# One-hot rows by pairs, padded relations, and repeated products in layer 0 of a four-layer graph network

## The chip, the core and the metric

The kernel runs on one core of one Trainium2 chip, in one launch. The metric is the device time of a run in microseconds; the median of three runs before the change is 5142.12 us. In the text PE is the tensor engine (products; PEld its loads of weights), DVE the vector engine, ACT the scalar engine, POOL the GpSimd engine, and SP the engine that issues plain DMAs.

## What is computed (the reference)

A graph of 3125 nodes with 128 features and 100,000 edges, sorted by their destination, goes through four layers. Each has the form x = layernorm(x + layer(x)). Cut to what matters here:

```python
# layer 0: attention over edges with relation types (500 relations, 64 numbers each), 8 heads
pre_edge = (h @ P1)[dst] + (h @ P2)[src] + (z @ P3)[edge_type]
logit_edge = leaky(pre_edge) @ y_w
alpha = softmax of the logits over the edges of a destination and the node itself
t_edge = (h @ Wh)[src] + (z @ Wz)[edge_type]
out = leaky(sum over edges of alpha * t_edge + residual_weight * h)
# layer 1: mean over neighbours, summed at the SOURCE of each edge, then two dense layers
agg = segment_sum(x[dst], src) / max(count of edges by src, 1)
# layers 2 and 3: attention with gathered keys and values
```

Layers 2 and 3 are not touched by the change.

## The kernel before, in words

The nodes are ordered by their number of incoming edges and cut into 25 tiles of 128, one node per partition. CAP gives the number of edge slots of each tile (57 down to 21, in all 821), W = 8 is a chunk of slots.

**Layer 0, the attention** (in tile_gnn, from about line 740). For each tile and each chunk of 8 slots, POOL gathers the rows of the source nodes into hs (one indirect DMA per slot, line 90; 8 buffers). Then one of two ways is taken, chosen by by_matmul. In gathered (line 801) the relation rows zs are gathered as well and added, and PE transposes the sum into pre (L815). In multiplied (line 819) the relation rows are made on PE: DVE compares a row of relation numbers with the partition numbers (oh, L834, bf16, 4 x 512), PE multiplies this one-hot with the table zq (L838) into zps, ACT copies it to zT (L839), PE multiplies zT with the weights into pre (L841) and adds the transposed hs (L843). The table zq holds the relation vectors in three bf16 parts, so that their sum is exact to fp32: parts 0 and 1 are one stationary operand of 128 columns, part 2 one of 64. In both ways logits (line 784) follows for each half chunk: DVE adds h1T (low, L787), ACT takes the relu (L788), PE multiplies by yw8 (lg, L790, four products). PE also makes t_ps (L849), which DVE adds to hs (L850). When all chunks of a tile are there, DVE does the softmax and the weighted sum over slots (L872, L796 to L799, L874), and the end of the tile makes x1 and its layer-1 product u.

**Layer 0, the counts.** Beside the attention runs the preparation of layer 1: counts (line 554) makes for each tile a 128 x 3200 matrix of how often each source node occurs. It is a generator, advanced by a share of its steps after each chunk. Its slots are first permuted: DVE makes one-hots ohb (L596) and oha (L600), ACT scales oha (L604, L605), PE multiplies them (c_perm, L608). Then, seven times per tile, DVE makes two blocks of one-hots, ohs and ohd (L623), by comparing numbers with the row up; PE multiplies them, 128 columns at a time (c_ps, L628), and ACT copies the result to cs (L630). All these one-hots are laid out as [partition, value, slot]: the 128 values of one slot lie 8 or 12 elements apart. The row c_up, made by count_up (line 539), holds the values 0 to 127, each 8 times, and fills one bank of PSUM (2 KB per partition).

The code is written in a framework that has its own scheduler: it decides the order of the instructions on each engine, from the dependencies and from priorities in the order of the program. It also sets all waits. It treats two accesses of different engines to the same PSUM bank as dependent, even where their bytes are apart. Each engine then takes its instructions in the built order.

Of the kernel before, what the change touches and what calls it, by code (L numbers as in the profile page):

```python
# [18 lines left out]
P = 128  # L19
# [15 lines left out]
R = 64  # L35
HC = 2 * D + H
NK = (PADREL + 1) // P
# [38 lines left out]
def tile_gnn(ctx, tc, a, out):  # L76
    nc = tc.nc
    V, A, G, T = nc.vector, nc.scalar, nc.gpsimd, nc.tensor
# [457 lines left out]
    V.tensor_copy(each_j, digits[:, :NT].unsqueeze(2).to_broadcast([P, NT, max(CAP)]))  # L536
    NAX = NT * max(NB)

    def count_up(pool, ps):

        up = ps.tile([P, P, SG], BF16, name="c_up")
        of = up.rearrange("p d s -> p (d s)")
        ri = pool.tile([P, 1], I32, name="c_ri")
        V.tensor_copy(ri, rowid)
        V.tensor_scalar(ri, ri, 3, None, op0=OP.arith_shift_right)
        rf = pool.tile([P, 1], F32, name="c_rf")
        V.tensor_copy(rf, ri)
        for k in range(SG):
            row = pool.tile([P, P], BF16, name="c_row", bufs=2)
            V.tensor_scalar(row, onesb, rf, float(k * P // SG), op0=OP.mult, op1=OP.add)  # L550
            T.transpose(of[:, k * P:(k + 1) * P], row, identb)
        return up

    def counts(t, cp, ps, up):

# [36 lines left out]
        perm = ps.tile([P, 2 * NAX], F32, name="c_perm", tag="c_ps")[:, :2 * NA]  # L592
        for s0 in range(0, n, SG):
            k = min(SG, n - s0)
            ohb = cp.tile([P, P, SG], BF16, name="c_ohb", bufs=2)
            V.tensor_tensor(ohb[:, :, :k], digb[:, 0, s0:s0 + k].unsqueeze(1).to_broadcast([P, P, k]),  # L596
                            up[:, :, :k], op=OP.is_equal)
            oha = cp.tile([P, SG * 2 * NAX], BF16, name="c_oha")[:, :SG * 2 * NA]
            oha = oha.rearrange("p (s e a) -> p s e a", s=SG, e=2)
            V.tensor_tensor(oha[:, :k, 1, :], digb[:, 1, s0:s0 + k].unsqueeze(2).to_broadcast([P, k, NA]),  # L600
                            digits[:, :NA].unsqueeze(1).to_broadcast([P, k, NA]), op=OP.is_equal)
            for s in range(k):
                o = OFF[t] + s0 + s
                A.activation(oha[:, s, 0, :], oha[:, s, 1, :], AF.Copy, scale=srclo[:, o:o + 1])  # L604
            A.activation(oha[:, :k, 1, :], oha[:, :k, 1, :], AF.Copy, scale=rowid)  # L605
            yield
            for s in range(k):
                T.matmul(perm, ohb[:, :, s], oha[:, s].rearrange("p e a -> p (e a)"), start=(s0 + s == 0),  # L608
                         stop=(s0 + s == n - 1))
        ends = cp.tile([P, 2, NAX], BF16, name="c_ends")  # L610
        V.tensor_scalar(ends[:, 0, :NA], perm[:, :NA], -1.0, None, op0=OP.add)
        A.activation(ends[:, 1, :NA], perm[:, NA:], AF.Copy)
        cs = cp.tile([P, NP], BF16, name="c_sb")
        for c in range(NCW):
            w = min(CW, NP - c * CW)
            n2, e0 = nb * w // P, nb * CW // P * c
            yield
            ohs = cp.tile([P, P, SE], BF16, name="c_ohs", bufs=2)
            ohd = cp.tile([P, P, SE], BF16, name="c_ohd", bufs=2)
            for b0 in range(0, n2, SG):  # L620
                b1 = min(n2, b0 + SG)
                for to, end in ((ohs, 0), (ohd, 1)):
                    V.tensor_tensor(to[:, :, b0:b1], ends[:, end, e0 + b0:e0 + b1].unsqueeze(1)  # L623
                                    .to_broadcast([P, P, b1 - b0]), up[:, :, :b1 - b0], op=OP.is_equal)
            cps = ps.tile([P, CW], F32, name="c_ps")
            for j in range(w // P):
                for i in range(nb):
                    T.matmul(cps[:, j * P:(j + 1) * P], ohd[:, :, nb * j + i], ohs[:, :, nb * j + i],  # L628
                             start=(i == 0), stop=(i == nb - 1))
# [118 lines left out]
    with tc.tile_pool(name="l0", bufs=2) as wp, tc.tile_pool(name="l0s", bufs=1) as sp, \  # L748
# [35 lines left out]
        def logits(pre, k, h1T, lg_ps):  # L784

            low = wp.tile([P, 4, P], F32, name="low")
            V.tensor_add(low[:, :k], pre[:, :k], h1T.unsqueeze(1).to_broadcast([P, k, P]))  # L787
# [13 lines left out]
        def gathered(h1T, idx, rl, n, za, lg_ps):  # L801

            hs = wp.tile([P, W, HC], F32, name="hs", bufs=8)
            zs = wp.tile([P, W, HC + R], F32, name="zs")
            for s in range(n):
                gather(hs[:, s, :], h_tab, idx(s))
                gather(zs[:, s, :], z_tab, rl[:, s:s + 1])
            V.tensor_add(hs[:, :n], hs[:, :n], zs[:, :n, :HC])
            halved(zs[:, :, HC:], n)
            V.tensor_add(za, za, zs[:, 0, HC:])  # L810
            for s0 in range(0, n, 4):
                k = min(4, n - s0)
                pre = ps.tile([P, 4, P], F32, name="pre")
                for s in range(k):
                    T.transpose(pre[:, s, :], hs[:, s0 + s, :D], ident)  # L815
                logits(pre, k, h1T, lg_ps[:, s0:s0 + k])
            return hs

        def multiplied(h1T, o, n, zbT, first, lg_ps):
# [8 lines left out]
            for s0 in range(0, n, 4):  # L828
                k = min(4, n - s0)
                cols = slice(s0 * P, (s0 + k) * P)  # L830
                oh = wp.tile([P, NK, 4 * P], BF16, name="oh")[:, :, :k * P]
                zps = ps1.tile([P, 4 * P], F32, name="zps")[:, :k * P]
                for i in range(NK):
                    V.tensor_scalar(oh[:, i], rb[:, cols], relid[:, i:i + 1], None, op0=OP.is_equal)  # L834
                    parts = [(zps, zq[:, i, :2 * R]), (zps[:R], zq[:, i, 2 * R:])]
                    for z, w in parts if i < NK - 1 else parts[::-1]:
                        whole = z is zps
                        T.matmul(z, w, oh[:, i], start=(whole and i == 0), stop=(whole and i == NK - 1))  # L838
                A.activation(zT[:, cols], zps, AF.Copy)  # L839
                pre = ps.tile([P, 4, P], F32, name="pre")  # L840
                T.matmul(pre[:, :k], zw[:, :D], zT[:, cols], start=True, stop=False)  # L841
                for s in range(k):
                    T.matmul(pre[:, s, :], hs[:, s0 + s, :D], ident, start=False, stop=(s == k - 1))  # L843
# [506 lines left out]
```

## Time and profile before

| | |
|---|---|
| three runs | 5137.88, 5142.12, 5148.45 us, median 5142.12 us |
| the profiled execution | 5814.11 us, its span 5812.4 us |
| busy in the span | PE 2236.2, PEld 1363.8, DVE 3104.1, ACT 934.1, POOL 3074.3 us |
| granted PE clock, mean of the span | 0.588 |
| stretch of layer 0 (210 to 3050 us of the span) | PE 1636, PEld 1070, DVE 1509, ACT 673, POOL 1403 us busy of 2840, granted clock 0.61 |
| c_ps products (L628) | 1300, of 128 columns |
| zps products (L838) | 752, of 512 columns |
| comparisons with c_up on DVE (L596, L623) | 114 and 386 in the trace, 0.68 us for 1024 elements |

All durations of single instructions come from the one profiled execution, which took 13% longer than the median of the runs. A line of groups has the source line, engine, operation, names of the tiles (written, then read), shape and count; then the busy time, the mean duration in ns, and the idle time of the engine before them with who ended it. A line of the timeline has start and duration in us, then the same names, and in brackets the idle time before it. A line of waits has the waiting instruction, the one waited for, the sum in us, the number and the longest. A line of stretches has the start and end, the length, then busy time and number of instructions of PE, PEld, DVE, ACT and POOL, the granted PE clock, the DMA share and GB/s. "remote" is a release that the trace gives to no instruction of this core; "issue" is idle time without a wait that it shows.

### The profile page before, as it was taken

The numbers are of one execution on the slowest core, as the hardware profiler recorded it, in microseconds if no ns is written. First come the engines' busy times: TensorE is split into PE (matmuls) and PEld (weight loads), VectorE is DVE, ScalarE is ACT, GpSimd is POOL, SyncE is SP. The second block draws the span as 40 slices with busy tenths as digits, with TensorE's granted clock in tenths as the row PEclk, the third lists the DMA queues.
The fourth block names the chain that finished last, engine by engine and source line by source line (L and its number), as shares of the span: only waits on it lengthen the run. The fifth ranks groups of instructions, "written<-read, shape, count | busy, mean of one in ns | idle before, by whom it ended". The sixth has DMA issues, their size and how long they took to land. (4 is left out here: it accounts for less than half of the span.)

```text
span 5812.4 us, 36204 instructions
## 1 busy us (share of the span) xinstructions
PE 2236.2 (38%) x10027; PEld 1363.8 (23%) x10027; DVE 3104.1 (53%) x6976; ACT 934.1 (16%) x2437; POOL 3074.3 (53%) x3136
## 2 busy tenths in 40 slices
PE   7165545555556556576658112222233200000000
PEld 5143333333334334344433001111111100000000
DVE  8354555554455446565652346565656455545555
ACT  1031222221222222222211001111111100000000
POOL 0555545545453544444640566566656366666664
PEclk9565556555665666566569555555555555555555
DMA  2423322322222222222335333333333233333332
GB/s 80 120 75 85 88 75 76 86 74 80 74 81 70 80 76 79 82 76 79 102 92 196 106 95 107 99 110 114 104 100 107 72 96 92 90 93 93 94 89 66
DMA packets 220239, 530.60 MB, mean 91 GB/s; under 512 B 65690, under 2 KB 112461, under 8 KB 215386
## 3 DMA queue, kind: packets, MB, share of 16 engines
q0 software_dynamic: 147968, 437.97, 26.6%
q1 hardware_dynamic: 72024, 89.90, 4.7%
q8 instruction: 87, 1.43, 0.1%
q14 instruction: 160, 1.30, 0.1%
HBM read 457.09 MB, written 70.63 MB: 91 GB/s over the span
## 5 line engine op out<-in xcount | busy, mean ns | idle before, releaser
L90 POOL DMA_INDIRECT hs<-h_tab,srcx x821 | 880.0, 1072 | 602.1 <-issue 448.7
L90 POOL DMA_INDIRECT kv<-kv_tab,pay_sb x821 | 782.1, 953 | 421.7 <-issue 239.5
L90 POOL DMA_INDIRECT kv<-ktv_tab,pay_sb x821 | 778.8, 949 | 332.3 <-issue 258.1
L90 POOL DMA_INDIRECT zs<-z_tab,rel x445 | 466.8, 1049 | 695.4 <-DVE az L810 303.3
L628 PE MATMUL c_ps<-c_ohs,c_ohd 128*128 128x128 bf16 x1300 | 334.3, 410 | 299.1 <-issue 110.3
L700 DVE TENSOR_REDUCE u<-msg 128x128 f32<-128x1024 f32 (+4 forms) x228 | 384.2, 1685 | 114.3 <-remote 69.6
L838 PE MATMUL zps<-oh,zq 128*128 128x512 bf16 x752 | 339.7, 516 | 88.3 <-DVE oh L834 80.1
L790 PE MATMUL lg<-yw,low 128*128 128x8 f32 x1642 | 306.4, 316 | 125.8 <-ACT low L788 81.6
L790 PEld LDWEIGHTS lg<-yw,low 128*128 128x128 f32 x1642 | 305.2, 276 | 162.8 <-ACT low L788 104.0
L628 PEld LDWEIGHTS <-c_ohd 128*128 128x128 bf16 x1300 | 187.2, 147 | 431.7 <-issue 256.2
L1295 DVE TENSOR_TENSOR qk<-kv,qp 128x1024 f32<-128x1024 f32 (+4 forms) x114 | 126.4, 1109 | 289.1 <-DMA kv<-ktv_tab,pay_sb 242.8
L623 DVE TENSOR_TENSOR c_ohs<-c_ends,c_up 128x1024 bf16<-128x1024 bf16 (+4 forms) x193 | 118.9, 616 | 248.0 <-remote 111.8
L696 DVE TENSOR_TENSOR msg<-kv,ex 128x1024 f32<-128x1024 f32 (+4 forms) x228 | 249.1, 1104 | 0.0
L604 ACT ACTIVATE c_oha<-c_oha,srclo 128x50 bf16<-128x50 bf16 (+2 forms) x821 | 201.5, 327 | 258.8 <-DVE c_oha L600 189.5
L850 DVE TENSOR_TENSOR hs<-hs,t_ps 128x408 f32<-128x408 f32 x141 | 74.5, 528 | 300.2 <-remote 193.0
L787 DVE TENSOR_TENSOR low<-pre,h1T 128x512 f32<-128x512 f32 (+1 forms) x215 | 141.3, 660 | 166.9 <-PE pre L843 76.1
L630 ACT ACTIVATE c_sb<-c_ps 128x512 bf16<-128x512 f32 (+1 forms) x175 | 96.5, 552 | 802.2 <-remote 363.0
L1143 DVE TENSOR_TENSOR qk<-kv,qp 128x1024 f32<-128x1024 f32 (+4 forms) x114 | 126.1, 1107 | 181.6 <-DMA kv<-kv_tab,pay_sb 173.1
L849 PE MATMUL t_ps<-zw,zT 128*128 128x136 f32 x752 | 153.7, 338 | 151.1 <-issue 105.1
L711 PE MATMUL tp<-ident,xk 128*128 128x128 f32 x100 | 42.3, 423 | 426.7 <-DVE xk L1211 88.6
L711 PE MATMUL tp<-ident,an 128*128 128x128 f32 x25 | 11.5, 461 | 434.5 <-DVE msg L696 174.3
L788 ACT ACTIVATE low<-low 128x512 f32<-128x512 f32 (+1 forms) x215 | 128.9, 606 | 274.7 <-DVE low L787 246.1
(394 smaller groups left out, 5252.7 us busy)
## 6 DMA issues: line engine op xcount, KB each, us to landing
c_tab<-c_sb SPq DMA_DIRECT2D x25, 768.0 KB
cs<-c_tab SPq DMA_DIRECT2D x6, 3200.0 KB
hs<-h_tab,srcx POOLq DMA_INDIRECT x821
kv<-kv_tab,pay_sb POOLq DMA_INDIRECT x821
kv<-ktv_tab,pay_sb POOLq DMA_INDIRECT x821
rb<-rel_tab SPq DMA_DIRECT2D x47, 256.0 KB
zs<-z_tab,rel POOLq DMA_INDIRECT x445
h_tab<-h SPq DMA_DIRECT2D x25, 132.0 KB
```

Of the source, the lines that this page charges most:

```text
L90: return G.indirect_dma_start(out=dst, out_offset=None, in_=table, in_offset=indirect(idx), **kw)
L604: A.activation(oha[:, s, 0, :], oha[:, s, 1, :], AF.Copy, scale=srclo[:, o:o + 1])
L628: T.matmul(cps[:, j * P:(j + 1) * P], ohd[:, :, nb * j + i], ohs[:, :, nb * j + i], start=(i == 0), stop=(i == nb - 1))
L696: V.tensor_tensor(msg[:, :n, :].rearrange("p s (h d) -> p s h d", h=heads), val.rearrange("p s (h d) -> p s h d", h=heads), ex.unsqueeze(3 ...
L700: V.tensor_reduce(u, msg[:, :n, :].rearrange("p s d -> p d s"), AX.X, OP.add)
L787: V.tensor_add(low[:, :k], pre[:, :k], h1T.unsqueeze(1).to_broadcast([P, k, P]))
L788: A.activation(low[:, :k], low[:, :k], AF.Relu)
L790: T.matmul(lg_ps[:, s, :], low[:, s, :], yw8, start=True, stop=True)
L838: T.matmul(z, w, oh[:, i], start=(whole and i == 0), stop=(whole and i == NK - 1))
L849: T.matmul(t_ps[:, s, :], zT[:, (s0 + s) * P:(s0 + s + 1) * P], zw[:, D:], start=True, stop=True)
L1143: V.tensor_mul(qk[:, :n], kv[:, :n, :D], qp.unsqueeze(1).to_broadcast([P, n, D]))
L1295: V.tensor_mul(qk[:, :n], kv[:, :n, :D], qp.unsqueeze(1).to_broadcast([P, n, D]))
```

## The change

Three edits, all in layer 0 and its preparation.

1. One-hots by pairs. The row c_up holds each value twice only (256 bf16), and the one-hots are laid out as [partition, pair of slots, value, slot of the pair]: the 128 values of one slot lie 2 elements apart. A new function one_hots makes them with one comparison for all pairs, and a second one for an odd slot.
2. Padded relations. zq gets 64 columns of zeros, so that part 2 is a stationary operand of 128 columns as well, and all eight products of a half chunk go into one accumulation over all 128 columns.
3. Repeated products. The rest of c_up's bank (384 fp32) becomes a target that nobody reads. The new function again multiplies an operand that PE has just used, its first 384 columns at most, with the identity into that target: four times after c_perm (over ohb), after c_ps (over ohs) and after zps (over oh); once over zT, over low after the logits, and over the last slot of hs in gathered (264 columns).

```diff
-    zq = const.tile([P, NK, 3 * R], BF16, name="zq")
+    zq = slots.tile([P, NK, 4 * R], BF16, name="zq")
+    G.memset(zq[:, :, 3 * R:], 0.0)
...
+    spare = []
+
     def count_up(pool, ps):
 
-        up = ps.tile([P, P, SG], BF16, name="c_up")
-        of = up.rearrange("p d s -> p (d s)")
+        bank = ps.tile([P, 8 * P], BF16, name="c_up")
+        of = bank[:, :2 * P]
+        up = of.rearrange("p (d s) -> p d s", s=2)
...
-        for k in range(SG):
+        for k in range(2):
             row = pool.tile([P, P], BF16, name="c_row", bufs=2)
-            V.tensor_scalar(row, onesb, rf, float(k * P // SG), op0=OP.mult, op1=OP.add)
+            V.tensor_scalar(row, onesb, rf, float(k * P // 2), op0=OP.mult, op1=OP.add)
             T.transpose(of[:, k * P:(k + 1) * P], row, identb)
+        spare.append(bank.bitcast(F32)[:, P:])
         return up
+
+    def again(rhs, k=1):
+
+        for _ in range(k if spare and rhs.shape[-1] else 0):
+            n = min(3 * P, rhs.shape[-1])
+            T.matmul(spare[0][:, :n], ident if rhs.dtype == F32 else identb, rhs[:, :n], start=True, stop=True)
+
+    def one_hots(to, nums, n, up):
+
+        for i, k, w in ((0, n // 2, 2), (n - n % 2, n % 2, 1)):
+            if k:
+                V.tensor_tensor(to[:, i // 2:i // 2 + k, :, :w], nums[:, i:i + k * w]
+                                .rearrange("p (b w) -> p b w", w=w).unsqueeze(2).to_broadcast([P, k, P, w]),
+                                up[:, :, :w].unsqueeze(1).to_broadcast([P, k, P, w]), op=OP.is_equal)
...
-                T.matmul(perm, ohb[:, :, s], oha[:, s].rearrange("p e a -> p (e a)"), start=(s0 + s == 0),
+                T.matmul(perm, ohb[:, s // 2, :, s % 2], oha[:, s].rearrange("p e a -> p (e a)"), start=(s0 + s == 0),
                          stop=(s0 + s == n - 1))
+            again(ohb.rearrange("p b d w -> p (b d w)")[:, :k // 2 * 2 * P], 4)
...
-            ohs = cp.tile([P, P, SE], BF16, name="c_ohs", bufs=2)
-            ohd = cp.tile([P, P, SE], BF16, name="c_ohd", bufs=2)
...
+            ohs = cp.tile([P, SE // 2, P, 2], BF16, name="c_ohs", bufs=2)
+            ohd = cp.tile([P, SE // 2, P, 2], BF16, name="c_ohd", bufs=2)
+            for to, end in ((ohs, 0), (ohd, 1)):
+                one_hots(to, ends[:, end, e0:e0 + n2], n2, up)
...
-                    T.matmul(cps[:, j * P:(j + 1) * P], ohd[:, :, nb * j + i], ohs[:, :, nb * j + i],
+                    b = nb * j + i
+                    T.matmul(cps[:, j * P:(j + 1) * P], ohd[:, b // 2, :, b % 2], ohs[:, b // 2, :, b % 2],
                              start=(i == 0), stop=(i == nb - 1))
+            again(ohs.rearrange("p b d w -> p (b d w)")[:, :n2 // 2 * 2 * P], 4)
...
                 T.matmul(lg_ps[:, s, :], low[:, s, :], yw8, start=True, stop=True)
+            again(low.rearrange("p k d -> p (k d)")[:, :k * P])
...
                     T.transpose(pre[:, s, :], hs[:, s0 + s, :D], ident)
+                again(hs[:, s0 + k - 1, :])
...
-                    parts = [(zps, zq[:, i, :2 * R]), (zps[:R], zq[:, i, 2 * R:])]
-                    for z, w in parts if i < NK - 1 else parts[::-1]:
-                        whole = z is zps
-                        T.matmul(z, w, oh[:, i], start=(whole and i == 0), stop=(whole and i == NK - 1))
+                    for k2 in range(2):
+                        T.matmul(zps, zq[:, i, 2 * R * k2:2 * R * (k2 + 1)], oh[:, i], start=(i + k2 == 0),
+                                 stop=(i == NK - 1 and k2 == 1))
+                again(oh[:, NK - 1], 4)
                 A.activation(zT[:, cols], zps, AF.Copy)
...
                     T.matmul(pre[:, s, :], hs[:, s0 + s, :D], ident, start=False, stop=(s == k - 1))
+                again(zT[:, cols])
```

More of the change, by code (lines that the diff above doesn't have):

```diff
@@ L537, in tile_gnn @@
     NAX = NT * max(NB)
+    spare = []
     def count_up(pool, ps):
-        up = ps.tile([P, P, SG], BF16, name="c_up")
-        of = up.rearrange("p d s -> p (d s)")
+        bank = ps.tile([P, 8 * P], BF16, name="c_up")
+        of = bank[:, :2 * P]
+        up = of.rearrange("p (d s) -> p d s", s=2)
         ri = pool.tile([P, 1], I32, name="c_ri")
         V.tensor_copy(ri, rowid)
-        V.tensor_scalar(ri, ri, 3, None, op0=OP.arith_shift_right)
+        V.tensor_scalar(ri, ri, 1, None, op0=OP.arith_shift_right)
         rf = pool.tile([P, 1], F32, name="c_rf")
         V.tensor_copy(rf, ri)
-        for k in range(SG):
+        for k in range(2):
             row = pool.tile([P, P], BF16, name="c_row", bufs=2)
-            V.tensor_scalar(row, onesb, rf, float(k * P // SG), op0=OP.mult, op1=OP.add)
+            V.tensor_scalar(row, onesb, rf, float(k * P // 2), op0=OP.mult, op1=OP.add)
             T.transpose(of[:, k * P:(k + 1) * P], row, identb)
+        spare.append(bank.bitcast(F32)[:, P:])
         return up
+    def again(rhs, k=1):
[8 more added lines that the diff above has]
+                                up[:, :, :w].unsqueeze(1).to_broadcast([P, k, P, w]), op=OP.is_equal)
     def counts(t, cp, ps, up):
@@ L594, in counts @@
             k = min(SG, n - s0)
-            ohb = cp.tile([P, P, SG], BF16, name="c_ohb", bufs=2)
-            V.tensor_tensor(ohb[:, :, :k], digb[:, 0, s0:s0 + k].unsqueeze(1).to_broadcast([P, P, k]),
-                            up[:, :, :k], op=OP.is_equal)
+            ohb = cp.tile([P, SG // 2, P, 2], BF16, name="c_ohb", bufs=2)
+            one_hots(ohb, digb[:, 0, s0:s0 + k], k, up)
             oha = cp.tile([P, SG * 2 * NAX], BF16, name="c_oha")[:, :SG * 2 * NA]
@@ L617, in counts @@
             yield
-            ohs = cp.tile([P, P, SE], BF16, name="c_ohs", bufs=2)
-            ohd = cp.tile([P, P, SE], BF16, name="c_ohd", bufs=2)
[L620 to L624, printed above, removed]
+            ohs = cp.tile([P, SE // 2, P, 2], BF16, name="c_ohs", bufs=2)
+            ohd = cp.tile([P, SE // 2, P, 2], BF16, name="c_ohd", bufs=2)
+            for to, end in ((ohs, 0), (ohd, 1)):
+                one_hots(to, ends[:, end, e0:e0 + n2], n2, up)
             cps = ps.tile([P, CW], F32, name="c_ps")
```

## The prediction

> **What bounds the kernel now.** I read the page's 40 slices first, to find where the tensor engine (PE) matters.
>
> ```profile
> PE   7165545555556556576658112222233200000000
> DVE  8354555554455446565652346565656455545555
> POOL 0555545545453544444640566566656366666664
> PEclk9565556555665666566569555555555555555555
> ```
>
> One slice is 145 us. Layer 0 fills slices 2 to 21. No engine is full there: PE and the vector engine (DVE) stand at 5 or 6 tenths, and the clock granted to PE is mostly half. After slice 22 PE is nearly idle, so a change of PE work can act in layer 0 alone. The table of stretches for layer 0:
>
> ```profile
> 210.00:3050.00 2840.00, 1636.26 (x7725) 1069.63 (x7724) 1508.60 (x3865) 672.82 (x1763) 1403.45 (x1338) 0.61 0.30 81
> ```
>
> Of 2840 us PE is busy 1636, DVE 1509, POOL 1403. The clock is 0.61; as it is granted as 0.50 or 1.00 in every short stretch I looked at, it was full for (0.61 - 0.50)/0.50 = 22% of the time. Layer 0 is therefore bound by hand-overs between engines that are each about half busy. The waits of DVE in the same stretch tell for whom:
>
> ```profile
> DVE hs L850 <- remote: 193.0, 15, 36.3
> DVE rest L985 <- ACT u L983: 146.0, 17, 31.7
> DVE c_ohs L623 <- remote: 111.8, 14, 17.9
> DVE c_ohs L623 <- PE c_ps L628: 90.5, 48, 19.9
> DVE low L787 <- PE pre L843: 76.1, 33, 27.8
> DVE hs L850 <- PE t_ps L849: 72.9, 47, 5.2
> DVE c_oha L600 <- PE c_perm L608: 67.3, 25, 36.7
> ```
>
> The lines of this view that name PE (these, c_oha<-zps 44.0, outdeg 25.6, lgs 22.0, low<-lg 20.6, c_ohs<-pre 18.2) sum to 437 us. "remote" lines (193.0, 111.8, 55.0, 54.6) add 414; they sit on instructions that read PE's results, and some matmul records are missing in such a trace, so I count them as probably PE. DVE thus waits 437 to 851 us for PE.
>
> Last, PE's own timeline, at places where the table of stretches gives a clock of 0.50 (c_ps at 1501, zps at 1534) or 1.00 (the others):
>
> ```profile
> 1501.04 2.05 PE L628 MATMUL c_ps<-c_ohs,c_ohd 128*128 128x128 bf16 x8 [1.76 <-DVE c_ohd L623]
> ...
> 972.16 2.02 PE L628 MATMUL c_ps<-c_ohs,c_ohd 128*128 128x128 bf16 x8
> ...
> 579.35 0.70 PE L608 MATMUL c_perm<-c_oha,c_ohb 128*128 128x150 bf16 x8
> ...
> 1534.58 3.23 PE L838 MATMUL zps<-oh,zq 128*128 128x512 bf16 x6 [12.34 <-DVE oh L834]
> ...
> 813.39 2.56 PE L838 MATMUL zps<-oh,zq 128*128 128x512 bf16 x8
> ```
>
> Eight count products (c_ps, 128 columns) take 2.0 us at either clock, while eight of 150 columns (c_perm) take 0.70. The first read their moving operand with a stride of 12 elements, the second without a gap. Products over relations (zps) do follow the clock: 0.538 us each at half, 0.320 at full.
>
> **What the Trainium skill says.** "TensorE: Matmul & The Clock Gate", Part 1, has two clocks only, released after about 3.4 us of sustained activity and lost after about as long idle; the trace agrees (0.50 and 1.00, a ratio of 0.538/0.320 = 1.7 for zps). "SBUF — State Buffer", at the end of its section Door 1, gives reads a 16-byte line: accesses that cross to a new line each time pay. The old stride is 24 bytes, the new one 4; the clock-blind 2.0 us of c_ps agrees. "TensorE: Matmul & The Clock Gate", Weight-path perf modes, wants 128 weights of a 16-bit type for the fast load; half of the zps loads have 64, and no run here shows yet that padding cures it. "PSUM — Partial Sum Buffer", PSUM bank collisions raise a hardware error, forbids two engines in one bank and quadrant at once: the build order shows the waits that follow from it.
>
> **The change part by part.**
>
> *One-hot rows by pairs.* DVE's work stays: a pair is still two adjacent 16-bit values, the 1024-element comparison took 0.68 us and keeps its count (92 of c_ohb, 126 instead of 144 of each of c_ohs and c_ohd, 18 of 1536 elements in place of a split; 17 odd remainders of 128 elements, a few us in all). I take DVE as unchanged; a lost packing would double 0.68 us in about 390 instructions, +260, which keeps one end of the range. On PE, c_ps falls from 2.02/8 = 0.252 us to that of c_perm scaled by 128/150: 0.70/8 x 0.85 = 0.075 at full clock and (an x8 run of 1.16 us at half clock) 0.124. I take 0.10: 1300 x 0.15 = 195 us less PE time. Bounds 0 and 230.
>
> *Padded relations.* 752 zps, each a load of about 0.12 us beside 0.2 or 0.43 of streaming. If the load hides as it does for c_perm, 752 x 0.1 = 75 us less; if not, nothing. I take 75. One memset on POOL before the layer: nothing, POOL waits there for loads.
>
> *Products repeated.* The built order has 1392 of 384 columns in bf16, 120 of 256 in bf16, 309 fp32 over low and zT (nearly all 384 columns) and 121 fp32 of 264. By column of c_perm (0.070 and 0.126 us from start to start for 150, an estimate from its x8 runs) a bf16 one of 384 costs 0.17 at full and 0.32 at half clock. By the fp32 pre product (two halves of 512 columns: 2.08 us at half clock, about 1.05 at full) an fp32 one costs 0.77 and 1.5, one of 264 columns 0.53 and 1.05. Sum: 554 us at full, 1055 at half clock.
>
> *The clock.* PE work that remains from before is 1636 - 195 - 75 = 1366 us. I take 30% of it as run at full clock (the 22% are dense stretches), and 60% afterwards, since the repeats fill gaps of 1 to 3 us but not the many of 5 to 20 us in which PE waits for gathers or for DVE's end of a tile. With a ratio of 1.75: 1366 x (0.4 + 0.6/1.75)/(0.7 + 0.3/1.75) = 1166 us, or 470 less than 1636, that is 29%. The repeats add 1055 x 0.4 + 554 x 0.6 = 754. PE is then busy 1920 us, more than before.
>
> *What lies on the path.* Real work that is 29% shorter shortens DVE's waits for PE by 29% of 437 to 851: 127 to 247, I take 180. The repeats stand in 423 runs (1.8 us each). After 366 of them PE's next real product has a wait of its own, which hides the run if it is long enough; after 57 it has none, and the run costs 57 x 1.8 = 103. I cost the 366 at nothing, covered by those waits (an activation of 0.6 us and an addition of 0.7 are typical); a tenth of them uncovered costs 66.
>
> *The wait that is added.* The repeats write the bank from which DVE reads c_up. So a comparison of the next step waits for the last repeat of the one before (208 comparisons wait so; before, 99 waited for c_ps, two steps back), and 110 runs of repeats wait for DVE. Behind DVE's wait stand the additions low and hs, and behind these PE's logits. A count step becomes a ring: 1.4 us on DVE, 0.9 of products, 0.7 of repeats, 0.2 of hand-over = 3.2 us at full clock against the 2.70 from one c_ps run to the next before; 0.5 us more on each of 175 steps would be 88 us, at half clock (1.0 + 1.3 + 1.4 + 0.2 = 3.9) 210. The build puts about 8 DVE and 24 PE instructions between two steps where there were 3 and 8, so I take nothing, and keep 210 for the range.
>
> Sum against the profiled execution: 5814 - 180 + 103 = 5737, 77 us less. The median shown is 5142, 0.884 of the profiled time, and the trace does not tell where the difference lies, so I scale: 77 x 0.884 = 68, **about 5070 us**.
>
> **Rivals.**
> - *Clock held nearly throughout.* All remaining work at full clock: 1366/1.75/0.871 = 896 us, 45% less; of 851 that is 383, less 60 for repeats: 323 x 0.884 = 286, about 4860. For it: the c_ps loops become dense. Against: 93 idle stretches of PE over 3.5 us, worked out from its records, stay.
> - *Repeats in the way: slower.* PE takes its products in the built order, so a run that outlasts the wait behind it delays real products, and through the shared bank DVE. If a third of the 366 runs are uncovered: 122 x 1.8 = 220, so +220 + 103 - 180 = +143, x 0.884 = 126, about 5268. It decides from 43 uncovered runs of 366 on (77/1.8), less where the clock stays at half. For it: PE's total rises from 1636 to 1920. Against: the placing just ahead of waits.
> - *Nothing.* Gathers and DVE's end of a tile set the pace (POOL waits 303 us for az L810, 448 for hs unnamed), and PE's gain only lengthens idle time: about 5142.
>
> **How the numbers follow.** Forecast 0.42 (4990 to 5130), clock held 0.18, slower 0.32, nothing 0.08. 0.2%, 10 us, is about what these runs can tell from no change. Faster: 0.40 of the forecast plus 0.18 and 0.02 of the rest = 0.60; same 0.08; slower 0.32. The range for 8 in 10 goes from 4880, short of the second case's best, to 5290, just past the slower case; the forecast's own is 4990 to 5130.
>
> **What would show it.** c_ps x8 near 1 us or below; zps near 0.22 us at full clock; layer 0's clock near 0.8; DVE's waits for c_ps and t_ps down by a third; PE busier, about 1900 us. Wrong: DVE waiting for c_up written by the repeats for over 150 us, comparisons near 1.3 us, or a clock that stays at 0.6.

## The result and the profile after

| | median | runs | ratio to before, 95% interval |
|---|---|---|---|
| before | 5140.9 us | 5137.88 to 5148.45 (4) | |
| after | 5444.74 us | 5430.76 to 5448.05 (4) | 1.0584 (1.0561 to 1.0606) |

The change makes the kernel 304 us slower. The profiled execution of after has a span of 5446.3 us, the same as its other runs. That of before, on which the prediction rests, was stretched as a whole (5812 us against 5141; layers 1 to 3, whose code is the same, took 2770 us there and 2521 here), so I took a second profile of before, called `b_again` below: its span is 5148.7 us, and it is the one to compare with.

The slices of after, 136 us each; layer 0 fills 2 to 21:

```profile
PE   7365555567665666776766702222333300000000
DVE  8455555566654565565744245665676445555566
POOL 0536455554655546445550177676777367777776
PEclk9676777778777787787877855555555555555555
```

The clock granted to PE rose from mostly 5 and 6 tenths to 7 and 8, and PE is fuller than before. DVE and POOL are not. The stretches of after (length, then busy time and count of PE, PEld, DVE, ACT, POOL, clock, DMA share, GB/s), split where layer 0 ends:

```profile
210.00:2925.00 2715.00, 1723.67 (x10090) 1190.24 (x10088) 1575.74 (x3831) 672.93 (x1757) 1418.08 (x1334) 0.77 0.31 84
2925.00:5446.00 2521.00, 491.71 (x1296) 207.78 (x1296) 1404.70 (x2629) 236.07 (x601) 1638.15 (x1719) 0.55 0.36 112
```

and of `b_again`:

```profile
210.00:2627.00 2417.00, 1593.15 (x7715) 1045.10 (x7713) 1507.20 (x3850) 671.65 (x1757) 1439.09 (x1334) 0.63 0.35 94
2627.00:5149.00 2522.00, 481.81 (x1296) 205.22 (x1296) 1403.89 (x2629) 236.01 (x600) 1638.25 (x1719) 0.55 0.37 112
```

The second lines agree within 1 us, so all of the loss lies in layer 0: 2715 - 2417 = 298 us. There the clock is 0.77 for 0.63, DVE is busy 69 us more, POOL does the same work. What grew is waiting. The waits of DVE in layer 0 of after, in order of size:

```profile
DVE hs L827 <- DMA zs<-z_tab,rel: 351.5, 15, 37.9
DVE hs L827 <- DMA hs<-h_tab,srcx: 218.2, 23, 22.5
DVE zs L815 <- DMA zs<-z_tab,rel: 160.4, 33, 19.5
DVE c_ohs L569 <- PE c_up L563: 87.0, 75, 5.7
DVE hs L871 <- PE t_ps L870: 60.2, 39, 11.7
DVE low L805 <- PE c_up L563: 41.4, 35, 4.2
```

and of `b_again`:

```profile
DVE c_oha L600 <- PE c_perm L608: 181.1, 34, 31.9
DVE c_ohs L623 <- PE c_ps L628: 164.6, 65, 25.9
DVE low L787 <- PE pre L843: 125.0, 39, 27.8
DVE hs L850 <- PE t_ps L849: 99.0, 66, 4.2
...
DVE hs L808 <- DMA zs<-z_tab,rel: 56.9, 5, 22.0
```

Summed over the whole view by what is waited for, DVE waited 741 us for PE and 91 for transfers before, and 378 and 733 after. So DVE's waits for PE halved, and waits for gathered rows took their place and more: -363 + 642 + 69 of work = 348, less 59 fewer waits for ACT, is 289 of the 298. (An engine's busy and idle time always fill the stretch, so this sum says where DVE's time went and not why.)

The waits are now at the addition of gathered rows (L827) and the halving behind it (L815), both in `gathered`. The timeline of DVE in after shows one such wait:

```profile
1503.22 0.14 DVE L990 TENSOR_SCALAR has<-deg_d 128x1 f32<-128x1 f32 x1
1503.28 0.14 DVE L991 TENSOR_SCALAR has<-deg_d 128x1 f32<-128x1 f32 x1
1503.34 0.20 DVE L591 TENSOR_TENSOR c_cnt<-c_end 128x25 bf16<-128x25 f32 x1
1531.56 2.36 DVE L827 TENSOR_TENSOR hs<-hs,zs 128x2112 f32<-128x2112 f32 x1 [28.02 <-DMA zs<-z_tab,rel]
1533.84 0.57 DVE L618 TENSOR_TENSOR c_oha<-c_digb,digits 128x400 bf16<-128x400 bf16 x1
1534.32 0.29 DVE L569 TENSOR_TENSOR c_ohb<-c_digb,c_up 128x128 bf16<-128x128 bf16 x1
1534.52 0.68 DVE L805 TENSOR_TENSOR low<-pre,h1T 128x512 f32<-128x512 f32 x1
1535.12 0.57 DVE L871 TENSOR_TENSOR hs<-hs,t_ps 128x408 f32<-128x408 f32 x1
```

DVE stands for 28 us at an addition whose gathers have not landed, and four instructions behind it then run without any wait of their own. "Perfetto Trace Analysis", Tensor Engine Instruction (MATMUL, LD_WEIGHTS), says that ACT, DVE and GPSIMD are strict FIFO, and this trace agrees: nothing passed the addition. DVE's place at the head of the queue is thus set by the order in which the program was built, and that order is what had changed. A simple measure of that order: the DVE records of layer 0 hold 67 additions of gathered chunks and 141 of products (L871). With each of them given to its own tile, the pairs in which a gathered addition runs ahead of a product addition of the same tile are 157 in before and 288 in after, of 387 possible. Below, "pairs" means this count. The expectations use another one, cut from one layer norm to the next (83 and 250), which the order in the traces does not give back; take their figures as rough labels.

POOL, which issues the gathers, waits in turn (after, layer 0):

```profile
POOL hs L90 <- DVE hs L818: 301.3, 9, 45.5
POOL hs L90 <- DVE az L895: 242.9, 11, 37.7
```

These name the end of `spread` (L895 and the halving L818 that it calls), which frees the eight hs buffers. DVE waits for gathers, POOL waits for buffers that DVE frees only later.

What the change was to do for PE it did. Groups of after (busy, mean ns of one; idle before and its releaser):

```profile
L645 PE MATMUL c_ps<-c_ohs,c_ohd 128*128 128x128 bf16 x1300 | 129.2, 250 | 257.5 <-DVE c_ohd L569 256.5
L856 PE MATMUL zps<-oh,zq 128*128 128x512 bf16 x752 | 220.3, 412 | 19.1 <-DMA rb<-rel_tab 14.2
```

of `b_again`:

```profile
L628 PE MATMUL c_ps<-c_ohs,c_ohd 128*128 128x128 bf16 x1300 | 334.2, 410 | 101.2 <-ACT c_sb L630 50.8
L838 PE MATMUL zps<-oh,zq 128*128 128x512 bf16 x752 | 336.0, 512 | 61.1 <-DVE oh L834 61.0
```

and of the changed kernel without its repeats (`e1_no_repeats`):

```profile
L856 PE MATMUL zps<-oh,zq 128*128 128x512 bf16 x752 | 270.9, 499 | 54.4 <-DVE oh L854 54.2
L645 PE MATMUL c_ps<-c_ohs,c_ohd 128*128 128x128 bf16 x1300 | 149.3, 274 | 132.1 <-DVE c_ohd L569 98.9
```

On the timeline of after eight c_ps took 0.62 us at full and 1.04 at half clock, where they took 2.0 at either, and four zps 1.03 at full clock:

```profile
1501.41 1.03 PE L856 MATMUL zps<-oh,zq 128*128 128x512 bf16 x4
...
1546.03 1.04 PE L645 MATMUL c_ps<-c_ohs,c_ohd 128*128 128x128 bf16 x8 [0.94 <-DVE c_ohd L569]
...
1555.03 0.62 PE L645 MATMUL c_ps<-c_ohs,c_ohd 128*128 128x128 bf16 x8
```

### The profile page after: what moved, and what is told of

Same layout as the page of the kernel before. It is cut to its first block, busy times and chain, and to the rows that moved or that the text cites. A ratio compares the mean times of both kernels' runs of the same rounds, so it can differ in the third digit from the quotient of the medians.

```text
span 5446.3 us, 40961 instructions
## 1 busy us (share of the span) xinstructions
PE 2325.8 (43%) x12393; PEld 1485.2 (27%) x12393; DVE 3143.4 (58%) x6949; ACT 933.4 (17%) x2437; POOL 3095.2 (57%) x3137
## 5 line engine op out<-in xcount | busy, mean ns | idle before, releaser
L90 POOL DMA_INDIRECT hs<-h_tab,srcx x821 | 913.8, 1113 | 996.5 <-issue 366.4
L827 DVE TENSOR_TENSOR hs<-hs,zs 128x2112 f32<-128x2112 f32 (+7 forms) x67 | 133.0, 1985 | 574.8 <-DMA zs<-z_tab,rel 351.5
L808 PEld LDWEIGHTS lg<-yw,low 128*128 128x128 f32 x1642 | 251.0, 227 | 151.6 <-ACT low L806 131.2
L808 PE MATMUL lg<-yw,low 128*128 128x8 f32 x1642 | 243.6, 275 | 107.3 <-ACT low L806 106.5
L645 PE MATMUL c_ps<-c_ohs,c_ohd 128*128 128x128 bf16 x1300 | 129.2, 250 | 257.5 <-DVE c_ohd L569 256.5
L563 PEld LDWEIGHTS <-identb 128*128 128x128 bf16 x1512 | 163.2, 114 | 274.2 <-issue 231.7
L856 PE MATMUL zps<-oh,zq 128*128 128x512 bf16 x752 | 220.3, 412 | 19.1 <-DMA rb<-rel_tab 14.2
L563 PE MATMUL c_up<-low,ident 128*128 128x384 f32 (+2 forms) x430 | 212.8, 582 | 0.0
L569 DVE TENSOR_TENSOR c_ohd<-c_ends,c_up 128x1024 bf16<-128x1024 bf16 (+4 forms) x178 | 198.7, 1117 | 0.0
L805 DVE TENSOR_TENSOR low<-pre,h1T 128x512 f32<-128x512 f32 (+1 forms) x215 | 141.2, 659 | 77.1 <-PE c_up L563 41.4
L645 PEld LDWEIGHTS <-c_ohd 128*128 128x128 bf16 x1300 | 101.0, 113 | 310.5 <-DVE c_ohd L569 294.3
```

The costliest lines, as they stand in the source:

```text
L90: return G.indirect_dma_start(out=dst, out_offset=None, in_=table, in_offset=indirect(idx), **kw)
L563: T.matmul(spare[0][:, :n], ident if rhs.dtype == F32 else identb, rhs[:, :n], start=True, stop=True)
L569: V.tensor_tensor(to[:, i // 2:i // 2 + k, :, :w], nums[:, i:i + k * w] .rearrange("p (b w) -> p b w", w=w).unsqueeze(2).to_broadcast([P, ...
L645: T.matmul(cps[:, j * P:(j + 1) * P], ohd[:, b // 2, :, b % 2], ohs[:, b // 2, :, b % 2], start=(i == 0), stop=(i == nb - 1))
L856: T.matmul(zps, zq[:, i, 2 * R * k2:2 * R * (k2 + 1)], oh[:, i], start=(i + k2 == 0), stop=(i == NK - 1 and k2 == 1))
```

## The experiments

Sixteen kernels ran. Each figure below is a median, with the 95% interval of its ratio to before. The texts of the first four were written before these letters were given; from `e4_thin` on they mean: A, the repeats change the order that the scheduler gives all queues, and DVE then stands at gathers; B, the time of the repeats on PE; C, the bank that they share with c_up.

### Before again, and the parts of the change

`b_again` is the kernel before, unchanged.

> The kernel before, unchanged, profiled once more. The first profile of it took 5814 us where its runs take 5141, and its layers 1 to 3, whose code is the same in both kernels, took 2770 us there and 2521 in the profile of the changed kernel. If that profile was stretched as a whole, this one should have about 5140 us, with layers 1 to 3 near 2520 and layer 0 ending near 2620 us instead of 3042. If the profiler itself slows this program, it will be near 5800 again.

5150.45 us in its one run, span 5148.7, with layer 0 ending at 2627 us and the rest taking 2522, as expected of a first profile that was stretched as a whole. Why that one was stretched stays open.

`e1_no_repeats`: pairs and padding stay, no product is repeated.

```diff
-        for _ in range(k if spare and rhs.shape[-1] else 0):
+        for _ in range(0):
```

> The changed kernel without the repeated products; pairs and padding stay. If the repeats and the waits that they bring through the shared bank cost the 304 us, it takes 5050 to 5140 us: the earlier 5141 less what the shorter c_ps (0.057 or 0.107 us from start to start against 0.232) and zps give. If the loss is in the new one-hots (c_ohd took 1.21 us against 0.81), or in an order of instructions that pairs alone bring, it stays above 5300.

5022.77 us, ratio 0.9762 (0.9746 to 0.9779). Pairs and padding by themselves gain 118 to 122 us; the repeats cost 5445 - 5023 = 422. Of the two cases expected the first came, 27 us below its range. Pairs and padding left the order nearly alone: in the traces 16 of POOL's 3137 instructions do not line up with those of `b_again`, against 586 between `e1_no_repeats` and after, and there are 153 pairs for 157.

`e11_pad_only`: the kernel before with the padded relations alone.

> The kernel before with the relations padded to four blocks of 64 columns alone: one-hot rows laid out as before, no repeats. 752 products of relations take about 105 ns less each, 79 us of PE time (with fewer still where the clock is granted). DVE's waits for what follows them are part of 741 us in layer 0. All theories: 5110 us (5080 to 5141); with the pairs it is 5023, so pairs would be worth the rest.

5108.51 us, ratio 0.9926 (0.991 to 0.9943): 36 us for the padding (zps 274.7 us busy for 336.0), and so 86 for the pairs on top of it.

`e3_even_ends`: in the changed kernel the second half of `ends` starts at element 75, or 150 bytes; here at 152.

```diff
-        ends = cp.tile([P, 2, NAX], BF16, name="c_ends")
+        ends = cp.tile([P, 2, NAX + NAX % 2], BF16, name="c_ends")
```

> The changed kernel with the row of ends padded from 75 to 76 numbers, so that the numbers for c_ohd start at a multiple of 4 bytes as those for c_ohs do. c_ohd should fall from 1.21 to 0.68 us; 150 comparisons then give up to 80 us. If DVE's time for the comparisons matters on the path, it takes 5360 to 5400 us; if not, 5440.

5424.86 us, ratio 1.0539 (1.0517 to 1.056), 20 below after. The comparison that writes c_ohd, in after:

```profile
L569 DVE TENSOR_TENSOR c_ohd<-c_ends,c_up x178: 291/1210/1747, 331.6 to 2809.3; 128x1024 bf16<-128x1024 bf16 x126, 128x256 bf16<-128x256 bf16 x24, 128x1536 bf16<-128x1536 bf16 x18, 128x512 bf16<-128x512 bf16 x6
```

and in `e3_even_ends` (ns: least, median, most):

```profile
L569 DVE TENSOR_TENSOR c_ohd<-c_ends,c_up x178: 254/679/948, 332.1 to 2792.5; 128x1024 bf16<-128x1024 bf16 x126, 128x256 bf16<-128x256 bf16 x24, 128x1536 bf16<-128x1536 bf16 x18, 128x512 bf16<-128x512 bf16 x6
```

1.21 us fell to 0.68. DVE is busy 1493 us instead of 1576, but only about 20 of these 83 us reach the end, between the two cases expected: DVE was waiting anyway.

### The bank

`e2_own_bank`: the row of values is copied to SBUF once, so comparisons no longer read the bank that the repeats write.

```diff
+        held = pool.tile([P, 2 * P], BF16, name="c_held")
+        V.tensor_copy(held, of)
...
-        return up
+        return held.rearrange("p (d s) -> p d s", s=2)
```

> The changed kernel with the row of values copied to SBUF once, so that the repeats write a bank that DVE never reads after the start. All 1942 repeats stay. If the waits through the shared bank (167 us of PE for c_ohb, 105 of DVE for c_up, and the order built around them) are the cause, it falls to 5150 or below. If it is the time of the repeats on PE, it stays near 5440.

5289.69 us, ratio 1.0285 (1.0268 to 1.0302): 155 below after, 267 above the kernel without repeats. The comparisons no longer wait for the repeats, and DVE still waits 644 us for transfers. This is neither of the two times expected. The built order changed here as well: the pairs are nearly the same (286 for 288), but 227 of POOL's 3137 instructions do not line up with those of after. So the 155 are not the bank alone.

### A forced order

`e6_gathers_first` has no repeats. An issue order like that of the changed kernel is forced on DVE's queue: gathered chunks are written in the program ahead of the later multiplied ones, and

```diff
-                V.tensor_add(hs[:, s0:s0 + k, D:], hs[:, s0:s0 + k, D:], t_ps[:, :k])
+                added = V.tensor_add(hs[:, s0:s0 + k, D:], hs[:, s0:s0 + k, D:], t_ps[:, :k])
+                for ins in held_back if not first else []:
+                    tc.add_manual_dep(added.ins, ins.name, mybir.DependencyInfo(mybir.DependencyClass.NoSync,
+                                      mybir.DependencyReason.DATA), reason="order")
```

(`held_back` holds the last addition of gathered rows.)

> The kernel without repeats, with an order forced on VectorE's queue only (no wait, no other work): in each tile the product additions of all multiplied chunks but the first are issued after the additions of the gathered chunks, as they stand in the changed kernel. Pairs of a gathered addition ahead of a product addition: 162 (79 without the forcing). Theory A: 5230 us (5150 to 5290), with VectorE waiting for gathers some 150 us more than there. Theories B and C: 5010 to 5050, as there are no repeats.

5125.57 us, ratio 0.9968 (0.9956 to 0.9981): 103 above `e1_no_repeats`, with no repeat in the program. DVE's waits for transfers rose from 76 to 261 us, those for PE fell from 605 to 510. The sign is A's and not that of B or C (5010 to 5050), but the time lies below A's range, though the pairs are 254 for 153. Nor did DVE's queue move alone: the scheduler built the other queues anew, and in the traces 544 of POOL's 3137 instructions do not line up with those of `e1_no_repeats`. So it shows what an order can cost without any repeat, and not that DVE's queue alone does it.

`e7_products_first` is the changed kernel with the same kind of edge the other way: the addition of gathered rows is issued after the last product addition that the program has before it.

> The changed kernel with all its repeats and the shared bank, and the opposite order forced on VectorE's queue: the addition of a gathered chunk is issued after the product additions of the multiplied chunk ahead of it. Pairs of a gathered addition ahead of a product addition: 97 (250 without the forcing). Theory A: most of the loss comes back, 5110 us (5050 to 5200) with the waits for gathers halved at least. Theory B: 5400 to 5450, since PE does the same work. Theory C: 5180 to 5445, as the bank's waits stay.

5257.30 us, ratio 1.0222 (1.0205 to 1.0239): 188 us come back from an edge that takes away no work and no wait. But 5257 lies outside A's range (5050 to 5200) and inside C's; DVE's waits for transfers are 472 us, for 733, and so not halved. The pairs are 45. Here too POOL's order moved (280 of 3137 against after).

`e8_own_order` has the row copied out and this edge; `e9_own_order_thin` in addition repeats of 8 columns.

> The changed kernel with both remedies: the row of values copied out, so that the comparisons don't read the bank that the repeats write (5290 us alone), and product additions forced ahead of gathered ones (5257 us alone, in the shared bank). All repeats stay. Pairs of a gathered addition ahead of a product addition: 65 (168 in the kernel with the row copied out, 250 in the changed one). Theory A, order and bank together make nearly the whole loss of 422 us: 5080 us (5030 to 5150). Theory B, the PE time of the repeats makes a good part by itself: 5180 to 5290.

> As the kernel with both remedies, with each repeat cut to 8 columns: the number of repeats stays, their PE time nearly goes. Pairs: 85, so that the order is close to that of the thick ones. What the thick ones take above this one is the price of their PE time with order and bank put right. Theory A: 5060 us, within 50 of the thick ones. Theory B: 5030 to 5060, over 120 below the thick ones.

5217.13 us, ratio 1.0142 (1.0125 to 1.0159), and 5161.42, ratio 1.0034 (1.0023 to 1.0046). A as I had put it fails here: 5217 lies in B's range. `e9_own_order_thin` is above the ranges of both; it is 56 us below the wide ones, which is A's difference (within 50) nearly, and half of B's. The largest wait of DVE in `e8_own_order` shows why:

```profile
DVE zs L817 <- DMA zs<-z_tab,rel: 349.4, 28, 47.6
```

The forced addition no longer stalls; the next instruction that needs the same gathers does. One edge moves the stand, it does not restore the order. The count of pairs tells one order from another, and does not price it: `e7_products_first`, `e8_own_order` and `e9_own_order_thin` all have 45, and all three are slower than `e1_no_repeats` with its 153.

### The width of the repeats

`e4_thin` cuts each repeat to 8 columns in the shared bank, `e10_own_thin` with the row copied out.

```diff
-            n = min(3 * P, rhs.shape[-1])
+            n = min(8, rhs.shape[-1])
```

> The changed kernel with each repeat cut from up to 384 columns to 8: their number, the bank that they write and the waits stay, their PE time nearly goes (output as the reference's). Theory A, the order of VectorE's queue: with repeats in the program the scheduler puts the additions of gathered chunks ahead of the products' additions, so VectorE stands at an addition whose gathers haven't landed. Counted over the tiles of layer 0, pairs of a gathered addition ahead of a product addition of the same tile are 83 in before, 79 without repeats (5023 us), 168 with the row of values copied out (5290), 250 in the changed kernel (5445), which is 2.5 to 3 us a pair; here the count is 161, so 5230 us (5180 to 5290). Theory B, the PE time of the repeats, behind which real products stand: the time goes nearly back to that without repeats, 5030 to 5100. Theory C, the shared bank alone: 155 above the kernel without repeats, about 5180.

> The row of values copied out and repeats of 8 columns, order left to the scheduler. Pairs: 118. Beside the thin repeats in the shared bank (5175 us, pairs 161) it shows the bank without their PE time. Theory A: 5120 us (5080 to 5160). Theory B: 5030 to 5070. Theory C, the bank alone: 5023 to 5040.

5174.91 us, ratio 1.0062 (1.0045 to 1.0079), and 5138.73, ratio 0.9988 (0.9979 to 0.9997). Narrow repeats give back 270 and 151 us of the wide ones' cost. They are not free of PE time, as I had expected: the groups of L563 sum to 313 us in `e4_thin`, 214 of them in fp32, against 781 in after. And the order differs again (197 and 186 pairs), because the scheduler plans with the time of each instruction. 5175 is what C gave and 5 us below A's range; 5139 lies in A's. So these two do not tell A from B.

### Order and width apart

The last four keep the order and change the width. A program was planned for one width, and its repeats were given the other width after the planning. Apart from the columns of the repeats every engine's instructions are the same, in the same order, as in the kernel with the same planning; the traces of each two have the same sequence on PE, ACT and POOL.

```diff
+            m = T.matmul(spare[0][:, :n], ident if rhs.dtype == F32 else identb, rhs[:, :n], start=True, stop=True)
+            AGAIN[m.ins.name] = min(3 * P, rhs.shape[-1])
...
+                if i.name in AGAIN:
+                    n = AGAIN[i.name]
+                    b.instructions[k] = copy.replace(i, outs=[widened(i.outs[0], n)], ins=[widened(i.ins[0], n), *i.ins[1:]])
```

(`widened` is the same access pattern with n columns; for the narrowed ones `n` and 8 change places. In `e12_own_wide_late` the repeats over gathered rows get 128 columns instead of 264, so that its 52 us below are a little low.)

> The repeats in a bank of their own. Every instruction stands in the order planned for repeats of 8 columns (5139 us), and the repeats are widened to up to 384 columns after the planning (those over gathered rows to 128, since the rest of a row is written later). With the order planned for wide repeats it is 5290. Theory A, the planned order costs the 151 us: 5110 to 5180, the higher clock perhaps giving some back. Theory B, the repeats' PE time costs it: 5260 to 5300.

> The other way about, in a bank of their own: the order planned for wide repeats (5290 us), in which repeats of 8 columns run. Theory A: 5260 to 5330, as the order stays and the clock falls. Theory B: 5130 to 5180, as the PE time goes.

> As the first of these, in the shared bank of the changed kernel: the order planned for 8 columns (5175 us), wide repeats (5445 with the order planned for them). Theory A: 5170 to 5250. Theory B: 5400 to 5450. Where the bank's waits grow with the repeats' time whatever the order, in between: 5250 to 5350.

> The order planned for wide repeats in the shared bank (5445 us), in which repeats of 8 columns run. Theory A: 5380 to 5450. Theory B: 5170 to 5230. Where the bank's waits grow with the repeats' time whatever the order, in between: 5280 to 5380.

| bank | order planned for | narrow repeats run | wide repeats run |
|---|---|---|---|
| own | narrow | 5138.73 (`e10_own_thin`) | 5190.70, 1.0093 (1.0076 to 1.0109) (`e12_own_wide_late`) |
| own | wide | 5302.45, 1.0306 (1.0288 to 1.0323) (`e13_own_thin_late`) | 5289.69 (`e2_own_bank`) |
| shared | narrow | 5174.91 (`e4_thin`) | 5264.33, 1.0225 (1.0204 to 1.0246) (`e14_wide_late`) |
| shared | wide | 5462.85, 1.0615 (1.0598 to 1.0633) (`e15_thin_late`) | 5444.74 (after) |

Read down a column, the order planned for wide repeats costs 164 and 99 us with an own bank, 288 and 180 in the shared one. Read along a row, the repeats' width costs 52 and 89 us in the order planned for narrow ones, and gains 13 and 18 in the other. In the changed kernel as built, cutting 470 us of repeats (781 in after, 311 in `e15_thin_late`) out of PE makes it 18 us slower. So between narrow and wide repeats the order is the larger part, and the time of the wide ones on PE, less what their clock gave back, is at most 89. Against the ranges, `e13_own_thin_late` is inside A's, `e12_own_wide_late` and `e15_thin_late` 11 and 13 us above it, and `e14_wide_late` in the stretch set for a bank whose waits grow with the width: part of its 89 may be the bank. The order here is that of all queues together; which queue's moves cost how much is not shown.

The waits say the same. DVE's in `e13_own_thin_late`, narrow repeats in the order for wide ones:

```profile
DVE hs L841 <- DMA zs<-z_tab,rel: 341.2, 16, 39.5
DVE hs L841 <- DMA hs<-h_tab,srcx: 203.3, 28, 19.9
DVE zs L829 <- DMA zs<-z_tab,rel: 90.2, 16, 11.1
DVE hs L885 <- PE t_ps L884: 70.2, 60, 7.2
```

and in `e12_own_wide_late`, wide repeats in the order for narrow ones:

```profile
DVE hs L885 <- PE t_ps L884: 175.3, 74, 14.7
DVE c_oha L632 <- PE c_perm L640: 106.3, 30, 26.6
DVE low L819 <- PE pre L877: 106.0, 26, 17.0
DVE c_ohs L583 <- PE c_ps L659: 91.5, 17, 23.8
DVE hs L841 <- DMA zs<-z_tab,rel: 77.9, 11, 12.1
```

DVE in layer 0, summed over each whole view (us):

| kernel | pairs | clock | DVE busy | waits for PE | for transfers |
|---|---|---|---|---|---|
| `e1_no_repeats` | 153 | 0.65 | 1551 | 605 | 76 |
| `e10_own_thin` | 186 | 0.63 | 1558 | 653 | 154 |
| `e12_own_wide_late` | 186 | 0.78 | 1558 | 732 | 134 |
| `e13_own_thin_late` | 286 | 0.63 | 1563 | 298 | 638 |
| `e2_own_bank` | 286 | 0.78 | 1562 | 293 | 644 |
| `e4_thin` | 197 | 0.64 | 1567 | 642 | 201 |
| `e14_wide_late` | 197 | 0.78 | 1567 | 764 | 168 |
| `e15_thin_late` | 288 | 0.63 | 1571 | 342 | 785 |
| after | 288 | 0.77 | 1576 | 378 | 733 |

The waits for transfers follow the planned order, and so does the fall of the waits for PE: it is there at a clock of 0.63 (342) as at 0.77 (378). The clock follows the width; in the orders for narrow repeats DVE waits longer for PE at 0.78 than at 0.63.

### The version that is faster than both

`e5_best`: no repeats, and `ends` lengthened by one.

> Pairs and padding without repeats, and the array of pair numbers lengthened by one so that the second comparison's numbers start at a multiple of 4 bytes. The order in the queues is that of the kernel without repeats. VectorE does 83 us less; it was the busiest engine there with 1551 us of 2295. Expected by all theories: 4990 us (4960 to 5020), some 30 below the 5023 without the lengthening; if VectorE isn't what the layer waits for, 5015.

4999.85 us, ratio 0.9718 (0.9702 to 0.9734), inside the range expected.

## Why the prediction was wrong

It said 5070 us, and 5445 came, outside its range and on the other side of before. The runs give the way there in steps: 5023 with pairs and padding alone, 152 more for narrow repeats in the shared bank (5175), 89 for their full width in that order (5264), and 180 for the order planned for wide ones (5445). (With the last two taken the other way about, it is 288 for the order and 18 less for the width.) The prediction's steps in turn:

- *DVE waits 437 to 851 us for PE.* Right: 741 in the undisturbed profile. *Layers 1 to 3 untouched.* Right. *Scaling by 0.884.* The first profile was stretched throughout, so a factor was the right kind of correction (layer 0 shrank to 0.85, the rest to 0.91).
- *c_ps 195 us less, zps 75 less.* Right: 334.2 - 149.3 = 185 and 336.0 - 270.9 = 65 without repeats. From start to start c_ps is now 57 ns at full and 107 at half clock, zps 216 and 427; "TensorE: Matmul & The Clock Gate", Wait — 56ns, not 53.3ns?, has 55.6 and 106.7, 215.7 and 426.7, so both now run at the array's own rate. The padding alone gave zps its 216 and 427 (`e11_pad_only`) and left c_ps at 233, so the new layout freed c_ps. That the 16-byte lines and the fast load are the mechanism fits, and no run here tells it from another.
- *I take DVE as unchanged.* Wrong in size: 1507 to 1576, as the comparison for c_ohd went from 0.81 us (not the 0.68 of c_ohs and c_ohb that was taken for all) to 1.21. In the changed kernel it cost about 20 us.
- *The repeats 754, layer 0's clock near 0.8, PE busy 1920.* Near for the first two, 781 and 0.77; PE was busy 1724 us.
- *Real work that is 29% shorter shortens DVE's waits for PE by 29%; I take 180.* Failed. Pairs and padding by themselves gave 118 to 122 at nearly the old clock (0.65 for 0.63), and the clock, with the repeats that hold it up, gave nothing: at one order, from 0.63 to 0.78, the waits for PE went from 653 to 732 and from 642 to 764. What the clock took off the real products, the repeats that bought it put back. That the two meet in the same waits is my reading; no run has the clock without the repeats.
- *I cost the 366 at nothing, and 57 at 103 us.* At one order the wide repeats cost 52 to 89 us in all over the narrow ones, whatever clock they bought. That is net of the clock, so it does not measure the terms one by one; as a sum, 91 us after scaling was about right.
- *The wait that is added: I take nothing, and keep 210.* The mark set for it, DVE waiting for c_up over 150 us, came: 87.0 + 41.4 + 33.1 + 17.6 = 179. Copying the row out gave 155 in the order for wide repeats and 36 in that for narrow ones, the orders differing too. (The ring's own sum is uneven: by the 0.075 and 0.124 us worked out before it, eight products are 0.6 and 1.0, not 0.9 and 1.0, so that 88 would be 35. The 210 stays.)
- The step that failed is the sentence on which this was put at nothing: *"The build puts about 8 DVE and 24 PE instructions between two steps where there were 3 and 8, so I take nothing"*. It saw that the build had moved instructions, and booked that as relief for one wait. It did not ask what else on those queues had moved. The additions of gathered rows had come ahead of the products' additions, among other moves, and the new order cost 180 us at the changed kernel's width, 288 at the narrow one. No term of the sum stood for it. How much of it those additions make, among the moves, is not shown.
- The rival *repeats in the way* had the sign right and the larger part of the cause wrong: its uncovered runs on PE are at most the 52 to 89 between narrow and wide, and what they are in the narrow ones is open. *DVE's waits for c_ps and t_ps down by a third* came true (164.6 and 99.0 to 60.2 for t_ps, with c_ohs now waiting 87.0 for c_up), but not by the clock: DVE stood at gathers instead. A mark that two mechanisms can make tells neither.

Open stays what the narrow repeats themselves cost, 116 us with an own bank and 152 in the shared one over the kernel without them. They bring some 310 us of PE work, an order of their own (186 and 197 pairs for 153, and 154 and 201 us of waits for transfers for 76) and, shared, the bank. Their removal in an unchanged order wasn't tried, since waits of other instructions hang on them. Open too is the releaser of waits of POOL that the trace gives as "issue", up to 42 us each.

## What to carry to other kernels

Where a scheduler places instructions by their planned time, filler on one engine can reorder every in-order queue, as it did here: compare the built order of all engines, above all what stands at the head of a queue ahead of a transfer, before counting the filler as free. A clock bought with filler must pay for the filler first: here it went from 0.63 to 0.78 at a loss of 52 to 89 us in one unchanged order, and a gain of 13 to 18 in another, in which DVE stood at gathers. To tell a cost of time from a cost of order, keep the order and change the time, and the other way about.

## What the runs showed of the hardware

- A comparison of two-element rows of 16-bit values, read by broadcast, took 1.21 us with its operand at 150 bytes and 0.68 at 152, for 1024 elements. The other operand lay in PSUM; with it in SBUF (`e2_own_bank`) the 1.21 stayed. "VectorE: DVE Perf Modes", Mode 2×_1P — pack two bf16 into one 32-bit read, asks for 4-byte alignment; "Vector Engine (DVE) Microarchitecture Reference" 5.1 Performance modes — why throughput varies by op and dtype, says that 4-byte alignment makes no difference. Here the start is all that differs, and it decides.
- Cutting a repeat to 8 columns saves more in bf16 than the length of its record says. The mean record in `e4_thin` is 0.17 us, against 0.36 to 0.41 in after at up to 384 columns, but from start to start the narrow ones mostly follow each other in 25 to 27 ns, the wide ones in 162 ns at full and 320 at half clock. In fp32 (two records a repeat) it saves less: the records of the narrow ones over low start mostly 213 or 111 ns apart, those of the wide ones 322 or 640.
